# Zeros between the rows of x2: laid in memory once, or put into the shifted tile by a second transfer

## The chip, the core and the metric

The kernel runs on one core of one Trainium2 chip. A core has five engines that run their own instruction streams in order and meet at semaphores: PE (matmuls, with its weight loads shown as PEld), DVE (vector work), ACT (activations and scaled copies), POOL (GpSimd) and SP (which here only issues transfers). All of this kernel's larger transfers go through SP's queue: a transfer that waits for something holds up every transfer behind it. Times are device microseconds (us) of one execution.

## The reference, cut to what matters

The input is 32 images of 192 channels and 56 by 56 pixels in float32. Four layers follow each other, each with a group normalisation (32 groups of six channels) ahead of it and an addition of its input behind it:

```python
x = x + L0(_gn(x), ...)   # agent attention, image by image
x = x + L1(_gn(x), ...)   # a recurrence (WKV) over the 3136 pixels, both ways
x = x + L2(_gn(x), offset)  # four channels at a time: shift, then a 3x3 filter
x = x + L3(_gn(x), ...)   # a long 55x55 filter for each channel, by FFT
```

L2 is the layer that the change touches. `offset` holds 48 pairs, one for every four channels. Each pair is rounded to whole pixels; the image is moved by that many columns and rows, and what comes in from outside is zero:

```python
R = round(offset)                       # 48 x 2
x_src = arange(W) - R[:, 0:1]           # columns; outside 0..W-1: zero
y_src = arange(H) - R[:, 1:2]           # rows; likewise
out = x[y_src, x_src] * mask
delta = offset - R
kern = exp(-((f + delta_x)**2 + (f + delta_y)**2) / (2 * 0.5**2)); kern /= sum
out = conv3x3(out, kern)                # separable, zero padding
```

Each offset component is between -96.5 and 96.5; a shift of 56 or more leaves nothing of the image.

## The kernel before, in words

The kernel has four stages, called from `all_blocks`.

`make_filter` computes L3's filters (`_rows_to_spectra` and products with Fourier matrices give their spectra). It calls `_find_shifts`, which turns `offset` into two small tables in memory: `taps` (for each of 48 positions the three column weights, three row weights and the row offsets) and `begins` (the column offset as an integer, `LEAD` minus the shift, with `LEAD` = 64).

`attention` runs over the 32 images and writes the result to the scratch tensor `x1` together with statistics for the next normalisation. `scan_pairs` computes L1 from `x1` and writes `x2`, stored by channel. `scan_guarded` stands behind a condition and replaces the scan where a value is out of range.

`channel_blocks` computes L2 and L3 together. It works by channel, not by image: a tile has 114 partitions (2 halves of the batch, 57 rows each, the 57th being a spare row of zeros) and 16 images of 56 columns along the free dimension. The 192 channels make 32 groups of six. For channel `c`, four channels ahead of its use, `prepare(c)` does the columns' part of L2:

- L1618 loads the channel into one of three tiles `shifted`, from an address that is `begins` elements off, so that the load itself moves the image by columns. This works because in memory each row of 56 pixels is followed by 56 zeros (`PITCH` = 112 columns): a row that is read off its place takes in zeros. The edge columns 0 and 57 of the tile are zeroed once.
- L1619, on POOL, multiplies by the normalisation's scale (`scale`, loaded at L1607).
- L1622, on ACT, makes the first of three tap products, `smooth`. Twice, L1625 on ACT makes another, `more`, and L1626 on POOL adds it to `smooth`.
- `matrix(i)` (L1567 to L1576), for every fourth channel, builds the 114 x 114 matrix `rows` that moves and weighs rows, on POOL, with one transposing product on PE.

`shift` (L1635 to L1643) loads the channel unmoved into `x`, multiplies `smooth` by `rows` on PE and adds the result on DVE. When a group's six channels are there, `middle` and `centre` (L1657 to L1664) give mean and squares, `spread` (L1669, L1670) gives the factor `rs`. Then `analyse` (L1683 to L1696, L1787, L1793) takes the channel to the frequency side and multiplies by the spectra `g`, and `synthesise` (L1709 to L1732) comes back and stores the output. The group that is analysed is one behind the group that is shifted; the loops at the end of `channel_blocks` interleave both.

The zeros between the rows are laid in `attention`: for each image, L869 writes the gaps of six channels from a tile of zeros (so 192 transfers for 192 channels), tied by a manual dependency behind that image's stores of `x1` (L863, L865). 64 zeros ahead of `x2` and 64 behind it are also written there.

The order of instructions on each engine is not simply the order of the source. A planner places them by readiness and priority; each engine, and SP's queue, then runs its list in order.

## Time and profile before

| What | us |
|---|---|
| median of three runs | 12223.14 |
| lowest and highest of the three | 12212.04, 12232.16 |
| the profiled execution's own time | 12216.98 |
| its span from first to last instruction | 12215.1 |
| gap writes (L869) of one image in SP's queue | 30.0 to 30.8 |
| first `rs` of the channel stage | 8545.5 |
| busy of PE, DVE, ACT, POOL | 11030.6, 10753.1, 7146.9, 3400.5 |

The granted clock of PE was 0.958 over the span. A line of a timeline gives start, length, engine, line, operation, output and inputs; in square brackets stands the idle time ahead of it with what ended it. `SPq` is SP's queue of transfers; the length of such a row is the time that the issuing took, not the time to landing. A row of waits gives engine, instruction and line, what it waited for, the total, how many times, and the longest. A row of windows gives the stretch, its length, and then the busy time (with the number of instructions) of PE, weight loads, DVE, ACT and POOL, the granted clock, the busy share of the DMA engines and GB/s.

### The profile page before, as it was taken

The numbers are of one execution on the slowest core, as the hardware profiler recorded it, in microseconds if no ns is written. First come the engines' busy times: TensorE is split into PE (matmuls) and PEld (weight loads), VectorE is DVE, ScalarE is ACT, GpSimd is POOL, SyncE is SP. The second block draws the span as 40 slices with busy tenths as digits, with TensorE's granted clock in tenths as the row PEclk, the third lists the DMA queues.
The fourth block names the chain that finished last, engine by engine and source line by source line (L and its number), as shares of the span: only waits on it lengthen the run. The fifth ranks groups of instructions, "written<-read, shape, count | busy, mean of one in ns | idle before, by whom it ended". The sixth has DMA issues, their size and how long they took to land. (4 is left out here: it accounts for less than half of the span.)

```text
span 12215.1 us, 157485 instructions
## 1 busy us (share of the span) xinstructions
PE 11030.6 (90%) x57358; PEld 6623.6 (54%) x57358; DVE 10753.1 (88%) x14722; ACT 7146.9 (59%) x14690; POOL 3400.5 (28%) x2568
## 2 busy tenths in 40 slices
PE   6999999999999999688888888886999999999999
PEld 3555555555555555333333333333666666666666
DVE  6888888888888888799999999996888899898897
ACT  3555555555555555466666666665666666666665
POOL 0000000000000000455555555555343343343330
PEclk9999999999999999899999999997999999999999
DMA  2222222222222222243334334334333333333331
GB/s 70 57 57 57 59 58 64 59 59 59 63 61 57 57 57 49 73 103 96 97 101 104 93 97 104 98 96 100 71 68 64 67 70 64 67 70 64 67 69 32
DMA packets 1959211, 876.56 MB, mean 72 GB/s; under 512 B 1821153, under 2 KB 1858292, under 8 KB 1949292
## 3 DMA queue, kind: packets, MB, share of 16 engines
q1 hardware_dynamic: 1948188, 840.69, 30.1%
q10 hardware_dynamic: 10240, 25.70, 0.8%
q8 instruction: 458, 7.50, 0.3%
q14 instruction: 325, 2.66, 0.1%
HBM read 482.13 MB, written 319.29 MB: 66 GB/s over the span
## 5 line engine op out<-in xcount | busy, mean ns | idle before, releaser
L619 DVE SCALAR_TENSOR_TENSOR o<-v_a,att_w,o 128x896 f32<-128x896 f32 (+1 forms) x1024 | 1056.8, 1032 | 467.3 <-ACT v_a L593 337.3
L1142 POOL MEMSET f<- 128x1 f32 x96 | 8.9, 99 | 4769.6 <-DMA st_c<-st 4764.6
L1793 ACT COPY y<-ps 64x252 f32<-64x252 f32 (+1 forms) x2376 | 808.7, 340 | 797.3 <-PE ps L1787 767.6
L1626 POOL TENSOR_TENSOR smooth<-smooth,more 114x896 f32<-114x896 f32 x384 | 866.3, 2259 | 1200.7 <-ACT more L1625 1141.2
L1709 PE MATMUL ps<-fixed,real 84*84 84x112 f32 x6144 | 1093.6, 260 | 0.0
L1709 PE MATMUL ps<-fixed,imag 84*84 84x112 f32 x6144 | 1091.1, 259 | 0.0
L1717 ACT ACTIVATE z<-ps,rs 84x112 f32<-84x112 f32 x3072 | 816.7, 355 | 322.1 <-PE ps L1709 319.5
L1709 PEld LDWEIGHTS ps<-fixed,real 84*84 84x84 f32 x6144 | 790.2, 154 | 158.4 <-issue 129.4
L1135 ACT ACTIVATE q<-q 128x784 f32<-128x784 f32 x384 | 328.5, 855 | 812.4 <-DVE q L1130 641.2
L1709 PEld LDWEIGHTS ps<-fixed,imag 84*84 84x84 f32 x6144 | 765.8, 153 | 0.0
L890 PE MATMUL ps<-sq,fixed 128*128 128x392 f32 x512 | 298.9, 746 | 425.9 <-ACT sq L1213 425.9
L636 ACT ACTIVATE pr<-ps,low 98x896 f32<-98x896 f32 (+1 forms) x384 | 352.3, 918 | 559.9 <-DVE low L634 559.9
L724 PE MATMUL ps<-gq_a,xs_a 128*112 128x294 f32 x1792 | 619.1, 427 | 45.7 <-DVE pq L729 45.7
L1787 PE MATMUL ps<-fixed,padded 114*128 114x168 f32 x3072 | 527.6, 322 | 134.6 <-DVE x L1729 118.3
L619 DVE SCALAR_TENSOR_TENSOR o<-v_c,att_w,o 128x448 f32<-128x448 f32 (+1 forms) x1024 | 638.3, 623 | 6.0 <-ACT v_c L604 0.9
L632 PE MATMUL ps<-xs_a,gk_a 128*98 128x448 f32 (+1 forms) x1536 | 637.1, 495 | 0.0
L633 PE MATMUL ps<-xs_c,gk_c 125*98 125x448 f32 (+1 forms) x1536 | 631.6, 492 | 0.0
L1728 PE MATMUL ps<-z,fixed 84*114 84x448 f32 x1536 | 609.7, 539 | 0.4 <-ACT z L1717 0.4
L725 PE MATMUL ps<-gq_c,xs_c 125*112 125x294 f32 x1792 | 608.3, 421 | 0.0
L890 PE MATMUL ps<-x,weights 128*128 128x392 f32 x1536 | 574.0, 517 | 31.1 <-DVE bv L1164 14.2
L737 ACT ACTIVATE pq<-pq 112x1176 f32<-112x1176 f32 x224 | 265.4, 1185 | 553.0 <-DVE pq L729 430.1
L1787 PEld LDWEIGHTS ps<-fixed,padded 114*128 114x128 f32 x3072 | 473.6, 198 | 206.1 <-DVE x L1729 140.5
(372 smaller groups left out, 29249.8 us busy)
## 6 DMA issues: line engine op xcount, KB each, us to landing
x<-x SPq DMA_DIRECT2D x576, 392.0 KB
x<-x SPq DMA_DIRECT2D x512, 196.0 KB
x<-zeros SPq DMA_DIRECT2D x192, 399.0 KB
shifted<-x SPq DMA_DIRECT2D x192, 399.0 KB
x<-x SPq DMA_DIRECT2D x192, 399.0 KB
out_x<-x SPq DMA_DIRECT2D x384, 196.0 KB
x<-in_x SPq DMA_DIRECT2D x32, 1568.0 KB
x<-x SPq DMA_DIRECT2D x32, 1568.0 KB
```

The lines of the kernel that those rows point to most:

```text
L619: nc.vector.scalar_tensor_tensor(dst, tap(i), dww[:, t, i : i + 1], dst, ALU.mult, ALU.add)
L632: mm(ps[P2, h, :n], g[:, cols], xs_a[j][:, px], start=True, stop=False)
L633: mm(ps[P2, h, :n], gk_c[0:KC, 2 * j + h, cols], xs_c[j][0:KC, px], start=False, stop=True)
L724: mm(ps[:SUB, i, :HA], xs_a[j][:, px], g, start=True, stop=False)
L725: mm(ps[:SUB, i, :HA], xs_c[j][0:KC, px], gq_c[0:KC, 2 * j + (q + i) // ns], start=False, stop=True)
L890: mm(out, aa, srcs[t][h], start=True, stop=False)
L1626: nc.gpsimd.tensor_tensor(y, y, more, ALU.add)
L1709: nc.tensor.matmul(ps[:84, i * 2 * S : (i + 1) * 2 * S], part[:, i0 + i].rearrange("p s u -> p (s u)"), f3[:, m, :], start=(m == 0), stop= ...
L1717: nc.scalar.activation(z[:, i0 + i].rearrange("p m w -> p (m w)"), ps[:84, i * 2 * S : (i + 1) * 2 * S], AF.Copy, scale=q.rs[:, i0 + i : i ...
L1728: nc.tensor.matmul(got, f4[:, m, :], z[:, i0 : i0 + n, m, :], start=(m == 0), stop=(m == 1))
L1787: nc.tensor.matmul(ps[:, g * 168 : (g + 1) * 168], flat[:, (g0 + g) * 128 : (g0 + g + 1) * 128], f1, start=True, stop=True)
L1793: nc.scalar.copy(y[64 * m : 64 * m + 64, 2 * g0 + i : 2 * (g0 + n) : 2], got[64 * i : 64 * i + 64, :, :, m, :])
```

## The change

The rows of `x2` lie next to each other in memory, 56 columns without a gap, and the tensor is half as large. The gap writes in `attention` are gone with their dependencies; the 64 zeros at either end are written in `_find_shifts`. A shifted load now takes in pixels of a neighbouring row where zeros should stand. So the tile `shifted` gets a row pitch of 112 columns again: the load puts 56 columns into each pitch, and a second transfer from a tile of zeros in SBUF covers 56 columns of each pitch from a place that is computed from `begins` in a register, which are just the columns without a source. POOL's scale comes after both. There are two such tiles in place of three.

Three smaller things come with it. `_find_shifts` is called after the sines of the filter network rather than ahead of them. The first two matrices of `matrix` are built on DVE instead of POOL. For channels 0, 2 and 4, the second and third tap are added by DVE in one operation each in place of ACT's copy and POOL's addition.

```diff
-PITCH = 2 * S
 LEAD = 64
...
-def _find_shifts(nc, cp, a, k, taps, begins):
+def _find_shifts(nc, cp, a, k, taps, begins, x2):
...
+    zeros = cp.tile([1, LEAD], F32, name="zeros", tag="zeros")
+    nc.vector.memset(zeros, 0.0)
+    for at in (0, x2.shape[0] - LEAD):
+        nc.sync.dma_start(out=x2[at : at + LEAD].unsqueeze(0), in_=zeros)
...
     beside()
-    _find_shifts(nc, cp, a, consts, *shifts)
...
     tc.add_manual_dep(loaded.ins, last.ins.name, behind, reason="the sines' set")
+    _find_shifts(nc, cp, a, consts, *shifts)
...
-    zeros = cp.tile([2 * (S + 1), LEAD], F32, name="zeros", tag="zeros")
-    for t in (*agents_b[0], *agents_b[1], v_a, v_c, zeros):
+    for t in (*agents_b[0], *agents_b[1], v_a, v_c):
         nc.gpsimd.memset(t, 0.0)
-    for at in (0, x2.shape[0] - LEAD):
-        nc.sync.dma_start(out=x2[at : at + LEAD].unsqueeze(0), in_=zeros[0:1])
...
-        for c in range(C * b // NB, C * (b + 1) // NB):
-            laid = nc.sync.dma_start(
-                out=gaps[c].rearrange("s h g w -> (s h) g w"),
-                in_=zeros[:, 0:S].unsqueeze(1).to_broadcast([2 * (S + 1), NB // 2, S]),
-            )
-            behind = mybir.DependencyInfo(mybir.DependencyClass.NoSync, mybir.DependencyReason.DATA)
-            tc.add_manual_dep(laid.ins, stored.ins.name, behind, reason="no burst")
...
-    shifted = [cp.tile([PR, NI, S + 2], F32, name=f"shifted{i}", tag=f"shifted{i}") for i in range(3)]
-    for t in shifted:
-        nc.gpsimd.memset(t[:, :, 0 : S + 2 : S + 1], 0.0)
+    shifted = [cp.tile([PR, 2 * S * (NI + 2)], F32, name=f"shifted{i}", tag=f"shifted{i}") for i in range(2)]
+    zeros = cp.tile([PR, S], F32, name="zeros", tag="zeros")
+    for t in (*shifted, zeros):
+        nc.gpsimd.memset(t, 0.0)
...
+            engine = nc.vector if n < 2 else nc.gpsimd
...
-                nc.gpsimd.tensor_scalar(
+                engine.tensor_scalar(
...
-            nc.gpsimd.tensor_tensor(t[0], t[0], t[1], ALU.add)
-            nc.gpsimd.tensor_tensor(mat, t[0], t[2], ALU.add)
+            engine.tensor_tensor(t[0], t[0], t[1], ALU.add)
+            engine.tensor_tensor(mat, t[0], t[2], ALU.add)
...
-    SPAN = PR * NI * PITCH
+    SPAN = PR * NI * S
...
-        t = shifted[c % len(shifted)]
-        there = flat_x2[bass.ds(begin_at[i] + c * SPAN, SPAN)].rearrange("(p g w) -> p g w", p=PR, w=PITCH)
-        nc.sync.dma_start(out=t[:, :, 1 : S + 1], in_=there[:, :, 0:S])
+        wide = shifted[c % len(shifted)]
+        t = wide[:, 2 * S - 1 : 2 * S - 1 + 2 * S * NI].rearrange("p (g w) -> p g w", w=2 * S)[:, :, 0 : S + 2]
+        there = flat_x2[bass.ds(begin_at[i] + c * SPAN, SPAN)].rearrange("(p g w) -> p g w", p=PR, w=S)
+        nc.sync.dma_start(out=t[:, :, 1 : S + 1], in_=there)
+
+        bare = wide[:, bass.ds(LEAD + S - begin_at[i], 2 * S * (NI + 1))].rearrange("p (g w) -> p g w", w=2 * S)
+        nc.sync.dma_start(out=bare[:, :, 0:S], in_=zeros.unsqueeze(1).to_broadcast([PR, NI + 1, S]))
...
+            if c < GROUP and c % 2 == 0:
+                nc.vector.scalar_tensor_tensor(y, t[:, :, f : f + S], taps[f], y, ALU.mult, ALU.add)
+                continue
...
-    n = C * 2 * (S + 1) * (NB // 2) * PITCH
+    n = C * 2 * (S + 1) * (NB // 2) * S
     x1, flat = scratch("x1", [NB, C, N]), scratch("x2", [n + 2 * LEAD])
-    wide = flat[LEAD : LEAD + n].rearrange("(c s h g w) -> c s h g w", c=C, s=2, h=S + 1, w=PITCH)
-    x2, gaps = wide[..., 0:S], wide[..., S:PITCH]
+    x2 = flat[LEAD : LEAD + n].rearrange("(c s h g w) -> c s h g w", c=C, s=2, h=S + 1, w=S)
...
-        make_filter(tc, a, k, filt, spectra, shifts, lambda: ready.load(nc, a, k))
-        attention(tc, a, ready, x1, st_a, st_c, flat, gaps)
+        make_filter(tc, a, k, filt, spectra, (*shifts, flat), lambda: ready.load(nc, a, k))
+        attention(tc, a, ready, x1, st_a, st_c)
```

More of the change, by code (lines that the diff above doesn't have):

```diff
@@ L407, in attention @@
 @with_exitstack
-def attention(ctx: ExitStack, tc: tile.TileContext, a, ready, x1, st_a, st_c, x2, gaps):
+def attention(ctx: ExitStack, tc: tile.TileContext, a, ready, x1, st_a, st_c):
     nc = tc.nc
@@ L864, in attention @@
         for h, r in HALVES:
-            stored = nc.sync.dma_start(
-                out=x1[b, 128:C, 1568 * h : 1568 * h + 1568], in_=x[1][r].rearrange("p y x -> p (y x)")
-            )
-        for c in range(C * b // NB, C * (b + 1) // NB):
-            laid = nc.sync.dma_start(
-                out=gaps[c].rearrange("s h g w -> (s h) g w"),
-                in_=zeros[:, 0:S].unsqueeze(1).to_broadcast([2 * (S + 1), NB // 2, S]),
-            )
-            behind = mybir.DependencyInfo(mybir.DependencyClass.NoSync, mybir.DependencyReason.DATA)
-            tc.add_manual_dep(laid.ins, stored.ins.name, behind, reason="no burst")
+            nc.sync.dma_start(out=x1[b, 128:C, 1568 * h : 1568 * h + 1568], in_=x[1][r].rearrange("p y x -> p (y x)"))
 class _Pairs:
```

## The prediction

> **What bounds the kernel now.** I read the page's engine totals first, then windows by stage, the chain of waits around the places that the change touches, and last the timelines of SP (its DMA queue), POOL, ACT and DVE there. The stages, from the windows and timelines: filter 0 to about 160 us, attention to 4923, scan to about 8434, channel blocks to the end.
>
> Engine totals of the page, then five stretches (core, then busy time with instruction counts of PE, weight load, DVE, ACT, POOL; granted clock, DMA share, GB/s):
>
> ```profile
> PE 11030.6 (90%) x57358; PEld 6623.6 (54%) x57358; DVE 10753.1 (88%) x14722; ACT 7146.9 (59%) x14690; POOL 3400.5 (28%) x2568
> ...
> 4940.00:4960.00 20.00, 0.00 (x0) 0.00 (x0) 0.00 (x0) 0.00 (x0) 0.00 (x0) 0.50 0.50 71
> ...
> 8444.00:8560.00 116.00, 43.37 (x102) 22.56 (x102) 41.86 (x51) 43.21 (x55) 94.69 (x80) 0.56 0.41 92
> ...
> 8700.00:12215.00 3515.00, 3370.68 (x19974) 2385.95 (x19972) 3110.20 (x4644) 2195.04 (x5925) 1253.15 (x711) 0.98 0.30 64
> ```
>
> PE and DVE bound the steady channel stage, ACT and POOL have room on average, the DMA engines more so. At 4940 every engine stands still for 20 us, and at 8444 POOL is the one that works. So three places matter: the end of attention, the first 100 us of the channel stage, and the 32 groups of it.
>
> SP's timeline at the end of attention (start, length, queue, line, transfer):
>
> ```profile
> 4926.92 1.23 SPq L865 DMA_DIRECT2D x<-x  x2
> 4928.19 30.03 SPq L869 DMA_DIRECT2D x<-zeros  x6
> 4958.33 5.58 SPq L936 DMA_DIRECT2D passing<-in_scan_o  x1
> ```
>
> The last image's six gap writes hold the queue for 30.03 us, and the scan's constants stand behind them. The waits between 600 and 5000 us name it twice:
>
> ```profile
> PE ps L955 <- DMA x<-zeros: 44.3, 1, 44.3
> ACT eu L969 <- DMA weights<-in_scan_w: 46.2, 1, 46.2
> ```
>
> The same gaps of an earlier image, in the middle of attention:
>
> ```profile
> 1094.87 30.79 SPq L869 DMA_DIRECT2D x<-zeros  x6
> 1125.70 6.18 SPq L392 DMA_DIRECT2D x<-in_x  x1
> ```
>
> Behind them stands only a later image's load, needed 60 us or more on, and in that stage's waits no engine waits for a DMA except at its end.
>
> The waits of 8700 to 12215 us that concern the shifted tile (total, times, longest):
>
> ```profile
> POOL shifted L1619 <- DMA shifted<-x: 443.8, 129, 7.5
> ...
> ACT more L1625 <- POOL smooth L1626: 85.1, 28, 5.0
> ...
> ACT more L1625 <- POOL shifted L1619: 68.3, 28, 2.6
> ```
>
> POOL's wait is idle time of a quiet engine. The other two stop ACT once a group each, about 2.4 and 3.0 us.
>
> One preparation, on SP and then POOL, and DVE at the start of the run:
>
> ```profile
> 9557.23 0.76 SPq L1618 DMA_DIRECT2D shifted<-x  x1
> ```
> ```profile
> 9563.51 1.74 POOL L1619 TENSOR_TENSOR shifted<-shifted,scale 114x928 f32<-114x928 f32 x1 [3.73 <-DMA shifted<-x]
> ```
> ```profile
> 56.82 0.21 DVE L218 TENSOR_SCALAR off<-off 114x96 f32<-114x96 f32 x1 [19.07 <-DMA off<-in_L_conv_offset]
> ```
>
> A shifted load lands about 6.2 us after its issue (9557.23 to 9563.51).
>
> **The skill's rule on the engines.** The Trainium skill, "SBUF — State Buffer", section "Who interferes with whom", says that a DVE instruction with two SBUF inputs and a GpSimd instruction that reads SBUF exclude each other for a whole instruction, while a reduction never contends. The trace agrees. The first fence is a stretch of a group without POOL work, the second one with it (by shape; count, busy us, mean ns, idle):
>
> ```profile
> L1692 DVE TENSOR_TENSOR real<-a,a 84x420 f32<-84x420 f32 x4 | 2.3, 582 | 0.0
> ```
> ```profile
> L1692 DVE TENSOR_TENSOR real<-a,a 84x420 f32<-84x420 f32 x6 | 6.1, 1016 | 0.0
> ```
>
> So POOL work put in a stretch where DVE is full costs DVE time. The change leaves POOL's scale and adds as many and as wide as before; only channels 0, 2 and 4 lose adds. The forecast takes no gain and no loss from it.
>
> **The change part by part**, against the profiled execution (12216.98 us; span 12215.1).
>
> *Gap writes gone (192 DMAs).* In steady attention they cost SP about 30.8 us an image with nobody late: 0. At the end, the loads of L936 to L942 follow the x1 stores. They still wait for those stores to land, which I put at 4932 to 4936, from some 5 us after 4926.92. Then the first starts about 1 us behind instead of at 4958.33: gain 24 to 30, taken as 29. Next late would be the scan's own load chain, the same as before and merely earlier.
>
> *`_find_shifts` moved in the source.* The instruction order of the changed kernel puts the `off` operation at the same place in DVE's stream, between the steps of the fifth sine, and SP's order up to its load (issued at 39.44, behind `xs_c`) is unchanged. So the 19.07 us stall stays. Two writes of 64 zeros and a small memset come in front of scan work that is far away. Gain 0 to 3, taken as 1.
>
> *Contiguous x load.* L1635 reads 114 rows of 3584 B instead of 1824 of 224 B. With the second transfer's 1938 runs of 224 B the packets per channel go from 1824 + 1824 + 1792 = 5440 to 114 + 1824 + 1938 + 1792 = 5668, at a DMA share of 0.30: 0.
>
> *Start of the channel stage.* In before, the first six products of L1641 begin at 8473.9, 8479.8, 8484.0, 8494.0, 8502.0 and 8510.1, and POOL carries them (94.69 of 116 us). After: tap matrices 0 and 1 go to DVE, and for channels 0, 2, 4 two DVE operations of about 1.03 us (the duration of a DVE operation of 114x896) replace two ACT copies of 1.04 and two POOL adds of 2.2. But each channel needs a load (6.2) and then the zeros' transfer before POOL's 1.74, with two tiles in place of three, so two channels take about 17.5 us. By hand the six come at about 8467, 8474, 8485, 8492, 8502 and 8510: earlier at first, equal at the sixth. The first spectra, queued behind them, come some 10 us sooner, and the later ones keep that. Gain 10, between a loss of 8 and a gain of 20. The wider memsets of POOL (two of 2016 columns) end before the first load lands.
>
> *The second transfer.* No row shows one from SBUF to SBUF. Nearest are the shifted load (6.2 us to landing, 3.7 each when back to back) and the gaps (about 5.1 each back to back, 30.79 for six). It can't take less than a load's fixed part, so I bound it by 4 and 7 us and take 6. SP waits for the load to land (6.2) before it may issue it, so a preparation goes from 6.2 + 1.8 = 8.0 us to 6.2 + 6 + 1.8 = 14. Behind SP's wait stand the output stores, the x loads (of which two or so are loaded ahead), the next shifted load and `g`. ACT's tap copies wait for POOL's scale.
>
> Six preparations make 6 x 14 = 84 us in a group of 114.7 us (the first `rs` at 8545.5, the 32nd at 12101.9, over 31): it fits, and two tiles overlap them. What counts is when ACT reaches the copies. At the group's start the two transfers miss ACT by 2 to 4 us, at three later preparations by 0.5 to 3, most of it beside PE work that is already queued: +0.5 to +2 a group on the path. Against this, in before the section that leads to `rs` (9570 to 9584.4) holds seven of ACT's tap copies (7.3 us), four batches of `z` (4.4) and the stall of 2.4; the order after has four copies there and none that waits for a fresh load: 3.1 + 2.4 = 5.5 us less on ACT. PE and DVE are full there too (15.0 and 14.6 of 15 us), so at most 0.5 to 2 a group of it is path. I take the two as equal: 0, with bounds of -3 and +4 a group.
>
> Sum: -29 - 1 - 10 + 0 = -40, so 12177 against the profiled execution. The median of the runs shown is 12223.14, 6 us above it: 12183.
>
> **The rivals.** About 0.2% (24 us) is what a measurement of this kernel tells from no change.
> - *A wait in place of the one removed (same).* The 40 us of the three ends are returned by the second transfer at 1.25 us a group (40 / 32). For it: three stalls of under 1 us do that. Against: SP's slack and ACT's 62% (2195 of 3515). Time 12223.
> - *ACT starved in every group (slower).* Place: the first preparation of a group, where ACT, in order, stands at a copy that waits for POOL's scale, with `z` and `y` copies behind it that feed PE. Price: the whole lengthening of 6 us less what the order lends, some 3.2 a group net, 32 x 3.2 = 102, so 12183 + 102 = 12285. It decides from a net 2 us a group (40 + 24 over 32). For it: two tiles instead of three, a wait in SP's only queue. Against: PE has queued work at that point.
> - *The section before `rs` really is ACT's (faster).* It gives the larger part of its 5.5 us, 3 a group over 31 groups: 93 more, 12090. For it: ACT stalls there each group. Against: PE and DVE read full.
> - *The moved call does remove the 19 us stall.* Then 12165. Against: the order of DVE.
>
> **How the numbers follow.** Forecast 0.42 (its own range 12150 to 12210), same by the returned wait 0.17, starved ACT 0.24, the `rs` section 0.13, the stall gone as well 0.04. Faster by over 0.2% is under 12199: most of the forecast (0.38), with 0.13 and 0.04, is 0.55. Within 0.2%: 0.17 and the forecast's upper edge, less the lower part of the starved case, 0.20. Slower: 0.25. The range 12095 to 12290 leaves out the tails of the third rival and of the starved one.
>
> **What would show it.** Right: no engine-wide silence at 4940 to 4960, and the scan's first load at about 4935; DVE's stall at `off` still about 19 us; first product of L1641 at about 8467 and the sixth near 8510; a group period of 114.7 within 0.5; ACT's waits for POOL's scale longer in the group's first copies, those before `rs` gone. The prediction is wrong if the period of a group moves by more than 1.5 us either way, or if the second transfer lands later than 7 us after its issue.

## The result, and the profile after

The changed kernel is slower: a median of 12297.85 us (12285.48 to 12300.92, six runs) against 12219.72 us of the kernel before in its six runs, a ratio of 1.0063 with a 95% interval of 1.005 to 1.0076. The forecast was 12183. The change gains more than was forecast before the channel stage, and loses all of it and more within that stage.

The page after, engine totals and the head of the chain that ended last:

```profile
PE 11099.2 (90%) x57358; PEld 6662.0 (54%) x57358; DVE 10776.0 (88%) x14739; ACT 7125.1 (58%) x14684; POOL 3379.2 (27%) x2551
...
PE 13%; DVE 7%; DMA 6%; ACT 3%; POOL 2%; issue 1%; SPq 0%; DVEq 0%; POOLq 0%; ACTq 0%
```

The same line of the chain on the page before:

```profile
PE 15%; DVE 12%; POOL 2%; ACT 1%; issue 1%; DMA 0%; DVEq 0%; SPq 0%; ACTq 0%; POOLq 0%
```

PE is busy 68.6 us longer for the same number of matmuls; the other totals hardly differ from before. The chain does: waits for a transfer to land had 0% of it before and have 6% now, the two of the shifted tile taking 3% each by the page's list of lines. A shifted tile that arrives late now lies on the chain that sets the end.

Where the time went is read from five marks in the two traces: the first and the last image's store of `x1`, the scan's first load, the first load of a shifted tile, and the first and last `rs` of the channel stage.

| Stretch | before, us | after, us | difference |
|---|---|---|---|
| up to the first image's store | 348.7 | 343.2 | -5.5 |
| 31 image periods | 4574.0 (147.55 each) | 4535.5 (146.31 each) | -38.5 |
| last store to the scan's first load | 35.6 | 5.7 | -29.9 |
| scan, to the first shifted load | 3491.9 | 3489.5 | -2.4 |
| first shifted load to first `rs` | 95.3 | 118.7 | +23.4 |
| 31 group periods | 3556.4 (114.72 each) | 3685.9 (118.90 each) | +129.5 |
| last `rs` to the end | 113.2 | 113.2 | 0 |

The sum is +76.6, the difference of the two spans (12291.7 and 12215.1). The first row isn't read as an effect: in kernels below whose code up to there is the changed kernel's, it lies between 343 and 357.

The end of attention after the change, SP's timeline:

```profile
4882.93 1.23 SPq L863 DMA_DIRECT2D x<-x  x2
4884.44 1.01 SPq L925 DMA_DIRECT2D passing<-in_scan_o  x1
```

The scan's first load follows the last store at once; the 30.03 us of gap writes are gone. At the start of the run the expected stall is still there:

```profile
57.16 0.21 DVE L216 TENSOR_SCALAR off<-off 114x96 f32<-114x96 f32 x1 [19.83 <-DMA off<-in_L_conv_offset]
```

One preparation of a channel after the change, from SP, then POOL, then ACT (with what ACT does next):

```profile
9573.21 0.86 SPq L1613 DMA_DIRECT2D shifted<-zeros  x1
```
```profile
9580.22 2.21 POOL L1614 TENSOR_TENSOR shifted<-shifted,scale 114x928 f32<-114x928 f32 x1 [8.52 <-DMA shifted<-zeros]
```
```profile
9573.00 4.23 ACT L1791 COPY y<-ps 64x252 f32<-64x252 f32 x12 [0.43 <-PE ps L1785]
9582.46 1.06 ACT L1617 ACTIVATE smooth<-shifted,found 114x896 f32<-114x896 f32 x1 [5.23 <-POOL shifted L1614]
...
9604.15 1.06 ACT L1617 ACTIVATE smooth<-shifted,found 114x896 f32<-114x896 f32 x1 [5.66 <-POOL shifted L1614]
9605.22 3.96 ACT L1715 ACTIVATE z<-ps,rs 84x112 f32<-84x112 f32 x16
```

The zeros land 7.0 us after their issue (9573.21 to 9580.22). Over the 8650 to 12090 us of the stage the median is 6.9 us, behind a load that takes 6.2 to 6.4. ACT stands idle 5.23 and 5.66 us at a first tap copy, and behind the second one stand sixteen `z` copies, which PE's products need. The sums for ACT after the change, between 8700 and 12000 us:

```profile
ACT smooth L1617 <- POOL shifted L1614: 438.5, 117, 7.3
...
ACT more L1623 <- POOL shifted L1614: 49.5, 28, 2.4
```

ACT's waits at the taps go from 153 us (85.1 and 68.3, two lines that the prediction shows) to 488 us (438.5 and 49.5) in some 28 groups: 12 us more in each. Not all of it lengthens the group, because ACT then waits less for PE at its `y` copies (402.6 us in this stretch against 651.6).

What reaches PE can be summed from the instructions and the clock records of the two traces, between the first and the last `rs`. PE stood still for 4.7 us of a group before and for 7.1 after, and the clock that it was granted stood at half for 3.9 us of a group before and for 6.9 after. So 2.3 of the 4.18 us that a group lost are pauses of PE. The other 1.8 are a longer busy time for the same matmuls, and the clock accounts for at most 1.5 of that, half of the 3.0 us more at half clock.

Attention's gain shows in DVE's timeline. First the kernel before, then after, in the same image:

```profile
1144.76 1.16 DVE L485 BATCH_NORM_STATS2 st_a<-x 128x6 f32<-128x448 f32 x2
...
1146.35 2.74 DVE L485 BATCH_NORM_STATS2 st_a<-x 128x6 f32<-128x448 f32 x5
```
```profile
1109.03 1.68 DVE L483 BATCH_NORM_STATS2 st_a<-x 128x6 f32<-128x448 f32 x3
...
1133.03 1.16 DVE L483 BATCH_NORM_STATS2 st_a<-x 128x6 f32<-128x448 f32 x2
...
1134.61 1.16 DVE L483 BATCH_NORM_STATS2 st_a<-x 128x6 f32<-128x448 f32 x2
```

Seven statistics operations on the first 128 channels of the next image stand together late before. After, the planner puts three of them some 25 us earlier, counted from the image's last store (at 1093.59 before, 1081.87 after).

### The profile page after: what moved, and what is told of

It is laid out like the page before. It is cut to its first block, busy times and chain, and to the rows that moved or that the text cites. A ratio compares the mean times of both kernels' runs of the same rounds, so it can differ in the third digit from the quotient of the medians.

```text
span 12291.7 us, 158148 instructions
## 1 busy us (share of the span) xinstructions
PE 11099.2 (90%) x57358; PEld 6662.0 (54%) x57358; DVE 10776.0 (88%) x14739; ACT 7125.1 (58%) x14684; POOL 3379.2 (27%) x2551
## 5 line engine op out<-in xcount | busy, mean ns | idle before, releaser
L1707 PEld LDWEIGHTS ps<-fixed,real 84*84 84x84 f32 x6144 | 793.8, 154 | 163.6 <-issue 131.8
L1614 POOL TENSOR_TENSOR shifted<-shifted,scale 114x928 f32<-114x928 f32 x192 | 362.8, 1889 | 1106.4 <-DMA shifted<-zeros 1070.0
L879 PE MATMUL ps<-x,weights 128*128 128x392 f32 x1536 | 573.2, 516 | 28.6 <-DVE bv L1153 14.3
```

The costliest lines, as they stand in the source:

```text
L879: mm(out, aa, srcs[t][h], start=True, stop=False)
L1707: nc.tensor.matmul(ps[:84, i * 2 * S : (i + 1) * 2 * S], part[:, i0 + i].rearrange("p s u -> p (s u)"), f3[:, m, :], start=(m == 0), stop= ...
```

## The experiments

Totals are medians, and each ratio is taken against runs of the kernel before in the same session (medians from 12219.72 to 12229.98 us). The other columns come from one trace each: "period" is the group period from the first to the last `rs`, "image" the image period, and "start" runs from the first shifted load to the first `rs`. behindx2 and best, whose channel stages have the same instructions in the same order, differ by 0.4 us in the period, so a smaller difference says nothing.

| Kernel | image | start | period | total | ratio to before (95%) |
|---|---|---|---|---|---|
| before | 147.55 | 95.3 | 114.72 | 12219.72 | |
| after | 146.31 | 118.7 | 118.90 | 12297.85 | 1.0063 (1.005 to 1.0076) |
| nobare | 146.29 | 88.9 | 122.00 | 12362.50 | 1.0109 (1.0093 to 1.0126) |
| ctrl | 146.32 | 120.5 | 118.77 | 12301.01 | 1.0061 (1.0045 to 1.0078) |
| three | 146.26 | 118.1 | 118.82 | 12293.56 | 1.0055 (1.0038 to 1.0072) |
| nobare3 | 146.31 | 81.5 | 114.32 | 12126.01 | 0.9921 (0.9904 to 0.9937) |
| two | 147.70 | 98.6 | 116.57 | 12283.40 | 1.0054 (1.0037 to 1.0071) |
| short3 | 146.26 | 90.9 | 113.12 | 12091.44 | 0.989 (0.9874 to 0.9907) |
| short2 | 146.29 | 100.6 | 113.35 | 12098.55 | 0.9896 (0.988 to 0.9913) |
| barepool | 146.16 | 164.5 | 131.78 | 12737.40 | 1.0427 (1.041 to 1.0444) |
| split3 | 146.31 | 109.6 | 119.68 | 12302.59 | 1.0058 (1.0041 to 1.0075) |
| mask | 146.31 | 99.2 | 119.31 | 12284.73 | 1.0047 (1.003 to 1.0064) |
| dest | 146.36 | 83.1 | 123.14 | 12387.20 | 1.0132 (1.0115 to 1.0149) |
| dest4 | 146.16 | 84.9 | 118.89 | 12261.04 | 1.0028 (1.0017 to 1.0039) |
| oldstart | 146.27 | 125.7 | 119.21 | 12303.94 | 1.0064 (1.0047 to 1.0081) |
| poolq | 148.50 | 94.6 | 114.68 | 12228.79 | 1.0006 (0.9997 to 1.0015) |
| gap4 | 154.11 | 95.4 | 114.32 | 12400.38 | 1.015 (1.0133 to 1.0167) |
| behindx | 147.30 | 94.7 | 114.62 | 12173.67 | 0.9957 (0.9941 to 0.9974) |
| behindx2 | 147.17 | 86.3 | 114.33 | 12160.81 | 0.995 (0.9933 to 0.9966) |
| best | 146.19 | 86.4 | 114.71 | 12130.48 | 0.9917 (0.9904 to 0.9931) |

### Without the second transfer (nobare)

```diff
-        bare = wide[:, bass.ds(LEAD + S - begin_at[i], 2 * S * (NI + 1))].rearrange("p (g w) -> p g w", w=2 * S)
-        nc.sync.dma_start(out=bare[:, :, 0:S], in_=zeros.unsqueeze(1).to_broadcast([PR, NI + 1, S]))
```

> The changed kernel without its second transfer: the zeros on columns without a source are left out, so those columns keep a neighbouring row's pixels. Two tiles, the pitch of 112, contiguous x2 and the start of the channel stage stay. Theory A (landing of the second transfer): each preparation loses its wait of about 7 us for the zeros, ACT's first tap copy no longer waits 5 us for POOL's scale, and the group period falls from 118.8 to between 113.5 and 115.5 us; the first rs comes 10 to 20 us sooner after the first shifted load (118.7 us in the changed kernel); total 12120 to 12200. Rival B (two tiles instead of three): the period stays at 117.5 or above and the total above 12240. Rival C (more bytes and packets on the DMA engines slow PE's and DVE's feed): the period falls in proportion to the DMA share, from 0.36 to about 0.26, by some 1 to 2 us, to about 117.

The period rose to 122.0. Both theories A and B in their simple form fail: taking the transfer away from this kernel makes the stage slower. ACT's waits for the tile are shorter in sum than in the changed kernel (273 us against 488) but stand at other copies:

```profile
ACT more L1621 <- POOL shifted L1612: 203.8, 53, 5.7
ACT smooth L1615 <- POOL shifted L1612: 69.3, 27, 3.5
```

The planner's order had changed with it: a copy of the next tile now stands between `rs` and the first `y` copies, on which PE depends.

```profile
9932.81 1.04 ACT L1621 ACTIVATE more<-shifted,found 114x896 f32<-114x896 f32 x1 [3.60 <-POOL shifted L1612]
9933.75 4.22 ACT L1789 COPY y<-ps 64x252 f32<-64x252 f32 x12
```

PE's clock is a part of it: it stood at half for 10.1 us of a group here, against 6.9 in the changed kernel.

### A control, and a third tile (ctrl, three)

ctrl:

```diff
-    xp = ctx.enter_context(tc.tile_pool(name="d_x", bufs=15))
+    xp = ctx.enter_context(tc.tile_pool(name="d_x", bufs=14))
...
-    padded = [cp.tile([PR, NI, 64], F32, name=f"padded{i}", tag=f"padded{i}") for i in range(8)]
+    padded = [cp.tile([PR, NI, 64], F32, name=f"padded{i}", tag=f"padded{i}") for i in range(7)]
```

three, on top of it:

```diff
-    shifted = [cp.tile([PR, 2 * S * (NI + 2)], F32, name=f"shifted{i}", tag=f"shifted{i}") for i in range(2)]
+    shifted = [cp.tile([PR, 2 * S * (NI + 2)], F32, name=f"shifted{i}", tag=f"shifted{i}") for i in range(3)]
```

> The changed kernel with seven padded tiles in place of eight and fourteen x tiles in place of fifteen, which frees the room for a third shifted tile in the next kernel. It is the control for that one. The instruction order of a group on ACT is the one of the changed kernel. Expected by every theory: group period 118.8 within 0.7 us, total 12285 to 12325.

> The control kernel with three shifted tiles: the second transfer stays, but the load of a channel may go out while two others are still being used. Theory A: the latency of load plus zeros (about 15 us up to the scale's end) can now be hidden by starting earlier only if SP gets there earlier; SP still stops at each zeros' transfer until its load has landed, so only part comes back: period 116 to 118. Rival B (the tiles are the cause): period back to 114.7 within 0.7 us, total about 12160 to 12190. If a third tile changes nothing (118.3 to 119.3), the two tiles have no part in it.

The control is the changed kernel within 0.13 us a group, and in the channel stage each engine runs its instructions in the changed kernel's order, so kernels built on it can be compared. A third tile changes nothing while the whole transfer is there (118.82 against 118.77).

### Neither the transfer nor the missing tile (nobare3), and two tiles before (two)

nobare3 joins the edits of nobare and three. two is the kernel before with one number changed:

```diff
-    shifted = [cp.tile([PR, NI, S + 2], F32, name=f"shifted{i}", tag=f"shifted{i}") for i in range(3)]
+    shifted = [cp.tile([PR, NI, S + 2], F32, name=f"shifted{i}", tag=f"shifted{i}") for i in range(2)]
```

> The changed kernel with three shifted tiles and without the second transfer (columns without a source keep a neighbour's pixels; seven padded tiles and fourteen x tiles as in the control). With the runs before it makes a square: transfer or not, two or three tiles. So far: transfer and two tiles 118.9 us a group, transfer and three 118.8, no transfer and two 122.0. Theory D (what counts is where ACT, in order, meets a tap copy whose tile isn't ready, with y and z copies behind it; either the transfer or the missing third tile makes it meet one): period 114.7 within 0.7 us, the total about 12219 - 44 - 30 = 12145. Rival E (something else of the change slows the stage: contiguous x loads, neighbouring rows in one transfer, the pitch of 112 in the tile): 117 or above.

> The kernel before with two shifted tiles in place of three, nothing else. Theory D: the period rises from 114.7 to 121 to 123 us, like the changed kernel without its second transfer, so the total is 12219 + 31 x 7 = about 12440. Rival E: the period stays under 116, total under 12260.

With both away the period is 114.32 and the total 12126, so nothing else of the change costs the stage anything that these runs can tell: not the contiguous `x` load, not the wide tile, not reading neighbouring rows. The square of four periods is 118.9 and 118.8 (transfer; two, three tiles), 122.0 and 114.3 (no transfer; two, three). In the kernel before, two tiles cost 1.85 us a group and not the 6 to 8 expected. A missing tile costs 7.7 us in one kernel and 1.85 in the other. The planner writes another order for each of the four, and the clock differs too (at half for 10.1 us of a group in nobare and 2.8 in nobare3, which can account for up to 3.7 of the 7.7), so it has no price of its own.

### The transfer cut to one row (short3, short2)

```diff
-        nc.sync.dma_start(out=bare[:, :, 0:S], in_=zeros.unsqueeze(1).to_broadcast([PR, NI + 1, S]))
+        nc.sync.dma_start(out=bare[:, 0:1, 0:S], in_=zeros.unsqueeze(1).to_broadcast([PR, 1, S]))
```

This stands on the changed kernel in short2, and on three in short3.

> The kernel with three shifted tiles and the second transfer, but that transfer carries only one row of 56 zeros for each partition (114 runs in place of 1938; the other columns without a source keep a neighbour's pixels). SP still stops for the load before it and POOL still waits for it. ACT's order in a group is that of the three-tile kernel with the whole transfer. If the time from issue to landing sets the loss (about 7 us for the whole transfer[...]), the period falls from 118.8 about in proportion, to 116 to 117. If it is the stop in SP's queue, it stays at 118 or above. If it is the bytes or the packets, it falls to 114.3.

> The changed kernel itself, two tiles and all buffers as they are, with the second transfer cut to one row of 56 zeros for each partition (the other columns without a source keep a neighbour's pixels). One size is changed. If the time that the zeros take to land sets the loss, the period falls from 118.9 to between 113 and 116 us, as it did with three tiles (118.8 to 113.1). If two tiles by themselves hold ACT's copies late, it stays at 118 or above, as without a transfer (122.0).

In short2, with every tile and wait of the changed kernel in place, the period falls by 5.55 us to 113.35, below the kernel before. SP and then POOL in short2:

```profile
9562.49 0.87 SPq L1610 DMA_DIRECT2D shifted<-x  x1
9569.05 0.77 SPq L1613 DMA_DIRECT2D shifted<-zeros  x1
```
```profile
9571.19 1.76 POOL L1614 TENSOR_TENSOR shifted<-shifted,scale 114x928 f32<-114x928 f32 x1 [5.80 <-DMA shifted<-zeros]
```

SP still stops until the load has landed (9562.49 to 9569.05), but the short transfer lands after 2.1 us (median 2.3). And ACT no longer waits at its first tap copies (0.4 us in all, where the changed kernel has 438.5); with the later copies, its waits for POOL's scale fall from 488 to 130 us:

```profile
ACT more L1623 <- POOL shifted L1614: 130.0, 57, 3.8
...
ACT smooth L1617 <- POOL shifted L1614: 0.4, 1, 0.4
```

The planner's order is a rival as the cause: it moved some of ACT's copies in short2. From the first group on, PE and DVE run the same instructions in the same order in after and short2, but ACT does not. The pair three and short3 decides. PE and DVE agree there as well, and in 17 of the 31 groups ACT's order is the same too; POOL and SP have single instructions in other places. In these 17 groups the period is 118.73 in three and 111.74 in short3. The same copy of one of these groups, in three and in short3:

```profile
9934.24 1.04 ACT L1623 ACTIVATE more<-shifted,found 114x896 f32<-114x896 f32 x1 [5.24 <-POOL shifted L1614]
```
```profile
9834.06 1.04 ACT L1623 ACTIVATE more<-shifted,found 114x896 f32<-114x896 f32 x1 [0.88 <-POOL shifted L1614]
```

The price has two parts. ACT waits for POOL's scale 3.8 us less in one of the 17 groups (1.3 against 5.1 on average), and over all groups PE's clock stands at half for 1.9 us of a group in short3 and 7.4 in three, which can account for up to 2.7 of the 5.7 us between their periods. That the clock falls because PE pauses is not isolated; in after, short2, nobare and nobare3 longer pauses and more time at half clock go together (7.1, 4.2, 8.9 and 4.7 us of pauses, 6.9, 2.8, 10.1 and 2.8 at half).

So it is not the second wait in SP's queue that costs the time but how long the whole transfer takes to land. Its bytes, its 1938 runs and its latency shrank together, so these runs don't say which of them makes it long, and they don't rule out that the traffic itself has a part in the price. With three tiles the expectation was 116 to 117 and the result 113.12: the loss does not fall in proportion to the landing, it is gone once the tile is there, or nearly there, when ACT asks.

### The wait moved to POOL's queue, and the loads asked for earlier (barepool, split3)

The column shift is loaded into a register of POOL as well.

```diff
...
-        nc.sync.dma_start(out=bare[:, :, 0:S], in_=zeros.unsqueeze(1).to_broadcast([PR, NI + 1, S]))
+        nc.gpsimd.dma_start(out=bare[:, :, 0:S], in_=zeros.unsqueeze(1).to_broadcast([PR, NI + 1, S]))
```

> The changed kernel with the second transfer issued from POOL's queue: the wait for the load's landing then stands in POOL, which has to wait for it anyway, and no longer in SP's queue ahead of the output stores, x loads and the next load. If SP's stopped queue is a part of the loss, the period falls below 118; if only the latency counts, it stays at 118 to 120. POOL's issue of such a transfer took 2.0 us in the run with the gap writes on POOL's queue, six times a group, so a rise to 121 would say that this issue is on the path too.

The period became 131.8. POOL itself now takes time for the issue and stands idle until the zeros are there:

```profile
9627.14 2.37 POOL L1613 DMA_DIRECT2D shifted<-zeros  x1 [0.94 <-DMA shifted<-x]
9639.81 1.75 POOL L1614 TENSOR_TENSOR shifted<-shifted,scale 114x928 f32<-114x928 f32 x1 [10.30 <-DMA shifted<-zeros]
```

From the issue to the scale 12.7 us go by (9627.14 to 9639.81), and 11.8 by the median, against 6.9 on SP's queue. A longer landing goes with a longer period here too, with the same bytes and runs, but POOL's own issuing has a part in it that was not separated, and PE's clock stood at half for 22.8 us of a group.

split3, on top of three:

```diff
+    def fetch(c):
...
     def prepare(c):
+        fetch(c + 1)
...
+    fetch(0)
     for c in range(4):
         prepare(c)
```

> The three-tile kernel with the whole second transfer, whose load and zeros are asked for one channel further ahead than POOL's scale and ACT's taps (five ahead in place of four). Nothing is left out. Theory D: the 15 us of load, zeros and scale are then over before ACT gets to the first tap, and the period returns to 114.3 to 115.5; total 12130 to 12170. If the transfer's traffic or SP's stops cost the time themselves, the period stays at 117.5 to 119, total 12250 or more.

The period was 119.68. The experiment did not do what it was meant to: the order in the source isn't the order in the queue, and the load and zeros stand no further ahead of POOL's scale than before. The scale still follows the load's issue by 12.7 us (9642.38 to 9655.08), with POOL waiting for the zeros. It says nothing about whether an earlier load would help.

### Zeros without a second transfer (mask, dest, dest4)

mask, with three narrow tiles as in the kernel before:

```diff
...
-        nc.gpsimd.tensor_tensor(t, t, _bc(scales[n][:, j], [PR, NI, S + 2]), ALU.mult)
+        both = wp.tile([PR, NI, S], F32, name="both", tag="both", bufs=1)
+        nc.gpsimd.tensor_tensor(both, _bc(scales[n][:, j], [PR, NI, S]), mask(i).unsqueeze(1).to_broadcast([PR, NI, S]), ALU.mult)
+        mid = t[:, :, 1 : S + 1]
+        nc.gpsimd.tensor_tensor(mid, mid, both, ALU.mult)
...
```

> Contiguous x2 as in the changed kernel, three narrow shifted tiles as in the kernel before, and no second transfer: POOL multiplies the scale by a row of ones and zeros ahead of the load's landing, and then multiplies the tile by that product, so the neighbour's pixels become zero. The price is one more POOL operation of about 1.8 us for each channel and three small ones for every fourth. Theory D: with no second landing ACT meets no late tile, the period is 114.3 plus what six more POOL operations cost DVE by their collisions: 115 to 117, total 12140 to 12220. If POOL or the collisions become the bound, 118 or above.

Here `mask(i)` is a row of ones and zeros made from the column shift for every fourth channel. The period is 119.31, above what was expected. The new POOL operation takes 2 us. DVE's additions that write `imag` take longer, most of all those of 84x504, six a group; first the kernel before, then mask:

```profile
L1696 DVE TENSOR_TENSOR imag<-a,a 84x504 f32<-84x504 f32 x172 | 122.1, 710 | 0.0
```
```profile
L1710 DVE TENSOR_TENSOR imag<-a,a 84x504 f32<-84x504 f32 x165 | 183.3, 1111 | 0.0
```

Six times 0.40 us are 2.4 us a group, and those of 84x420 (1058 ns on average against 983, some twelve a group) add 0.9. In all DVE is busy 3.1 us a group longer than in nobare3, of the 5.0 that separate mask from it. How much of this lies on the path was not isolated: PE pauses only 1.8 us a group longer than in nobare3, and its clock stands at half for 9.1 us against 2.8.

dest:

```diff
...
-        nc.sync.dma_start(out=t[:, :, 1 : S + 1], in_=there)
...
+        view = wide[:, 2 * S : 2 * S + 2 * S * NI].rearrange("p (g w) -> p g w", w=2 * S)[:, :, 0:S]
+        if c % 4 < 2 and c > 1:
+            nc.gpsimd.memset(view, 0.0)
+        put = wide[:, bass.ds(LEAD + 2 * S - begin_at[i], 2 * S * NI)].rearrange("p (g w) -> p g w", w=2 * S)
+        nc.sync.dma_start(out=put[:, :, 0:S], in_=x2[c].rearrange("s h g w -> (s h) g w"))
+        t = scaled[c % len(scaled)]
+        nc.gpsimd.tensor_tensor(t[:, :, 1 : S + 1], view, _bc(scales[n][:, j], [PR, NI, S]), ALU.mult)
...
```

> Contiguous x2 and no second transfer: the load takes each row whole and puts it at a computed place in a tile with a pitch of 112, so that it falls with its shift into columns that are zero. POOL scales from there into a second narrow tile with fixed zero edges, and clears the wide tile (static columns, a write of about 1 us) when the shift changes, twice in four channels. Seven padded and fourteen x tiles as in the control. The load's tile is free once it is scaled and not only after the taps. By theory D no tap meets a late tile: period 113 to 115.5 us, start 80 to 92, total 12090 to 12150. If POOL's clearing delays the load or collides with DVE, 116 or above.

The period is 123.14, although no second transfer is waited for. ACT waits for POOL's scale again:

```profile
ACT smooth L1619 <- POOL scaled L1616: 219.5, 52, 4.2
```

dest4 has three tiles `scaled` in place of two, and thirteen x tiles in place of fourteen.

> The kernel that puts rows at a computed place, with three scaled tiles in place of two and thirteen x tiles in place of fourteen. With two scaled tiles the period was 123.1, and ACT's taps waited for POOL's scale, which waits for the taps of the channel two before. If that is the missing third tile, as in the run without second transfer (122.0 with two tiles, 114.3 with three), the period falls to 113.5 to 115.5 and the total to 12090 to 12150. If the clearing of the wide tile or its load's place is the cause, it stays above 118.

It gives 118.89, above the 118 that the expectation sets for the clearing or the load's place as the cause. Even so the third tile goes with 4.3 us a group less; as much again is not explained (the clearing, the fewer x tiles, the order and the clock were not separated). None of the three kernels beats the kernel before.

### The start of the channel stage undone (oldstart)

```diff
-            engine = nc.vector if n < 2 else nc.gpsimd
+            engine = nc.gpsimd
...
-            if c < GROUP and c % 2 == 0:
+            if False:
```

> The changed kernel with the start of the channel stage undone: the first two matrices on POOL again, and the second and third taps of channels 0, 2 and 4 by ACT and POOL. From the first shifted load to the first rs the changed kernel takes 118.7 us and the kernel before 95.3. By the prediction's account the DVE work saves some 10 us there: 128 here, total about 12307. If the two transfers in series are all that counts at the start, 119 and no change. The group period stays at 118.9.

The start is 125.7 us, so the DVE work of the change saves 7.0 us. The shortened transfer of short2 brings the start from 118.7 to 100.6, so 18.1 us at the start go with the size of the zeros' transfer.

### Attention: traffic or order (poolq, gap4, behindx, behindx2, best)

poolq:

```diff
-            laid = nc.sync.dma_start(
+            laid = nc.gpsimd.dma_start(
```

> The kernel before with its 192 gap writes issued by POOL's queue in place of SP's, nothing else changed. The planner's order of DVE in attention then becomes that of the changed kernel (three of the five statistics operations on the next image's first half stand some 35 operations earlier), while the same bytes are still written. Theory O (order): the image period falls from 148.2 to 146.8 us as in the changed kernel. Theory T (traffic): the writes themselves slow attention, and the period stays at 148.2. Either way SP's queue is free at the end of attention, so the scan's first load follows the x1 stores by about 2 us and not by 31. Channel stage unchanged, period 114.7. Total by O 12219 - 41 - 30 = 12148, by T 12189. If POOL's own descriptor work is slow, its last six writes may still hold back POOL's first operations of the scan.

The image period was 148.5, which looked like theory T. The mean misleads. From the eleventh image to the thirtieth the period is 146.79 on average, as in the changed kernel (146.74; 148.18 before). All of the excess lies in the first ten (153.6), where PE waits for a table, `gk_c`, for 2 to 11 us in eight images. So this run supports theory O as well. POOL needs 2.04 us to issue one such write, and the scan took 10 us longer (3502 us), which stays open:

```profile
1078.28 2.05 POOL L869 DMA_DIRECT2D x<-zeros  x1 [3.77 <-issue]
```

gap4:

```diff
-        for c in range(C * b // NB, C * (b + 1) // NB):
+        for c in range(6 * b, 6 * b + 4):
             laid = nc.sync.dma_start(
...
-        there = flat_x2[bass.ds(begin_at[i] + c * SPAN, SPAN)].rearrange("(p g w) -> p g w", p=PR, w=PITCH)
+        at = begin_at[i] + c * SPAN if c % 6 in (1, 2, 3) else LEAD + c * SPAN
+        there = flat_x2[bass.ds(at, SPAN)].rearrange("(p g w) -> p g w", p=PR, w=PITCH)
```

> The kernel before with four gap writes for each image in place of six; the zeros for two channels of six are left out, and three channels of six are not shifted by columns so that no gap is read that wasn't written. Only attention and its end are of interest. The planner's order on DVE becomes the changed kernel's (three statistics operations earlier), while two thirds of the writes stay on SP. Theory O (order): image period 146.3. Theory T (traffic): 147.55 less a third of 1.24, 147.1. End of attention: the scan's first load follows the last x1 store by 20 us in place of 30.

The image period was 154.1, outside both expectations, and the waits of attention say why:

```profile
DVE st_a L485 <- DMA x<-in_x: 201.5, 27, 10.2
```

The planner put the three statistics operations early, as in the changed kernel, but the next image's load still stands behind four gap writes in SP's queue. DVE waits 7.5 us for it in every image. So the early place needs the load to be early.

behindx lays the gaps behind that load (and the last image's with the image before it):

```diff
             nxt = ready.image(nc, a, b + 1)
+            for c in range(6 * b, 6 * b + (12 if b == NB - 2 else 6)):
+                laid = nc.sync.dma_start(
...
+                tc.add_manual_dep(laid.ins, ready.last.ins.name, behind, reason="behind the load")
...
-        for c in range(C * b // NB, C * (b + 1) // NB):
-            laid = nc.sync.dma_start(
```

behindx2 adds the changed kernel's two DVE edits at the start of the channel stage.

> The kernel before with each image's six gap writes put behind the load of the next-but-one image in SP's queue and not ahead of it, and the last image's six moved to the image before it. The bytes, packets and number of writes stay. The planner then gives DVE the changed kernel's order (three statistics operations earlier). If the gain of 1.24 us an image came from that order and from the load being early enough for it, the image period is 146.3 and the scan's loads follow the last stores by about 2 us: total 12219 - 39 - 30 = 12150. If the traffic of the writes itself slows attention, the period stays at 147.5 and the total is 12189.

> The same with the changed kernel's start of the channel stage (two matrices on DVE, taps of channels 0, 2 and 4 on DVE). From the first shifted load to the first rs 95.3 us become 81 to 85, as in the run with three tiles and no second transfer (81.5): about 12 us less than the kernel with the gap writes behind the load, 12138.

The image period of 147.3 holds one wait of PE, for a table that stood behind twelve gap writes:

```profile
PE ps L725 <- DMA gq_c<-once: 28.6, 1, 28.6
```

One wait of 28.6 us is 0.92 us of each of 31 images; without it the period is 146.4. The start of behindx2 is 8.4 us shorter than behindx's (86.3 and 94.7).

best is behindx2 with those last six writes laid in the first image instead, behind its table:

```diff
                 gq = seen(ag, wqT, gq_c, "gq_a")
+                for c in range(C - 6, C) if b == 0 else ():
+                    laid = nc.sync.dma_start(
...
+                    tc.add_manual_dep(laid.ins, ready.once.ins.name, behind, reason="behind the spread")
```

> The kernel before with the gap writes behind the next image's load, the last image's six laid in the first image (behind its second table, where SP's queue was empty for some 120 us), and the changed kernel's start of the channel stage. In the run with twelve writes in the last image but one, a table stood behind them and PE waited 28.7 us once; that wait goes. Image period 146.3, group period 114.3, start 86, total 12160.8 - 29 = about 12132. If the image period stays at 147, the traffic of the writes costs time after all.

SP in the middle of attention in best:

```profile
1089.18 1.24 SPq L878 DMA_DIRECT2D x<-x  x2
...
1094.35 1.14 SPq L394 DMA_DIRECT2D x<-in_x  x2
1095.55 35.22 SPq L811 DMA_DIRECT2D x<-zeros  x6
```

All 192 writes are still there, and the image period is 146.19. In an image in the middle, best, behindx and gap4 run PE's, ACT's and DVE's instructions in the changed kernel's order; the kernel before differs from it on DVE alone, by the three statistics operations and one operation on `got`. Theory O holds: the writes' traffic costs nothing that is seen here, their place ahead of the next image's load did. best takes 12130.48 us, a ratio of 0.9917 (0.9904 to 0.9931) to the kernel before, and is faster than both kernels.

## Why the prediction was wrong

- **Gap writes at the end of attention: right in size.** 29 us were forecast, 29.9 came (35.6 to 5.7 us between the last store and the scan's first load). The step had the load wait until the stores had landed, at 4932 to 4936, which by its own times gives 21 to 25 us. No such wait came: the load was issued 1.5 us behind the last stores (4882.93 and 4884.44).
- **Gap writes in steady attention: wrong.** The step said "with nobody late: 0". It read only which engine waits for a transfer, and it took the load behind the writes to be needed 60 us or more later; DVE's first statistics operation on that load ran 19 us after its issue (1125.70 and 1144.76). The 30.79 us ahead of the next image's load kept no engine waiting because the planner had already put seven statistics operations late, behind that load. With the load early, three of them fill a place 25 us sooner: -1.24 us an image, -38.5 in all. behindx and best show it with the traffic left in. The order of DVE's instructions in the changed kernel shows the move; the prediction speaks of that order only at `off`.
- **`_find_shifts` moved: right.** The stall at `off` is 19.83 us, 19.07 before.
- **Contiguous x load: right, at nothing.** nobare3, which keeps it, has a period of 114.32.
- **Start of the channel stage: wrong in sign.** Forecast -10 (with -20 to +8), measured +23.4. The DVE part was about right: it saves 7.0 us with the transfer (oldstart) and 8.4 without it (behindx2 against behindx). The step that failed is "two channels take about 17.5 us", which let the first `rs` come sooner. After the change a pair took 21.6 to 24.6 us (POOL's scales at 8388.64, 8410.27, 8434.33 and 8458.94), and the sixth product of L1639 came 73.6 us after the first shifted load, where the forecast's 8510 against 8450.2 makes 60. Without the whole transfer the start is 18.1 us shorter (short2).
- **The second transfer, steady: wrong.** Its landing was put at 6 us between 4 and 7 and took 6.9 (median), so that part was near. The step that failed is "most of it beside PE work that is already queued: +0.5 to +2 a group". It costs 5.55 us a group (118.90 against 113.35 in short2): PE pauses longer, and its clock, which the step left out, stands at half for longer. The other half of the step fits but is not isolated: the order with fewer tap copies ahead of `rs` was credited with 0.5 to 2 us, and short2, which has the wait nearly gone, lies 1.4 us below the kernel before. The sum of the two is +4.18, just outside the bounds of -3 and +4, and over 31 groups 129.5 us.
- **The rivals.** "ACT starved in every group" named the place and the mechanism, at 3.2 us a group; 4.18 were measured. It was given 0.24, with "PE has queued work at that point" against it. But ACT runs in order, and the `y` and `z` copies that make PE's next work stand behind the copy that waits. That the total (12297.85) is so near that rival's 12285 is partly luck: attention's extra gain of 38.5 us hides more than half of what it undervalued in the stage (129.5 against 102 us) and at its start (33 us). Of the other side's rival, that the section before `rs` is ACT's alone, at most a part is seen: the 1.4 us of short2, of the 3.

What stays open: why two tiles without any transfer are worse (122.0) than two tiles with it (118.9), beyond that the planner's order differs and sets other copies ahead of `y`, and that the clock's longer half time can account for up to 1.6 of the 3.1 us; what in the shortened transfer, its runs or its bytes, made it land early; and what holds dest4 at 118.9.

## What to carry to other kernels

A transfer that is added behind another one lengthens the chain of the tile by its time to landing, also where the DMA engines have room (a share of 0.36 in the groups here): ask which in-order engine meets that tile first, and what stands behind the meeting instruction. And a transfer that nobody waits for may still be the reason why others were put late: where a planner sets the order, removing it moves instructions on engines that never touch it, and that move has to be read from the new order, engine by engine, before the change is costed at nothing. Before removing work from a queue, try its other side: here the same 192 writes, laid behind the load instead of ahead of it, gave all that the change had gained in attention, without the second transfer.

## What the runs showed of the hardware that was not expected

A transfer from SBUF to SBUF of 424 KB in 1938 runs of 224 B landed 6.9 us after its issue (median), no sooner than the load of 399 KB in 1824 runs from memory (6.2 to 6.4), while one of 114 runs landed after 2.3. The Trainium skill, "DMA: Bandwidth & Descriptors", section "Why small descriptors are slow (HBM only)", says that transfers between SBUF and SBUF don't suffer the penalty of small descriptors; no advantage over the load from memory is seen here, though these runs don't separate runs from bytes. And issuing such a transfer from POOL's queue occupied POOL for 2.04 us (1824 runs) and 2.37 us (1938 runs), where the second transfer's issue took SP 0.8 to 0.9 us when nothing held its queue.
